# A selective-scan stage rebuilt in tiles of 32 channels by four states

## The chip, the cores and the metric

The kernel runs on one NeuronCore of a Trainium2 chip. The metric is the device time of one launch in microseconds (us). Five engines work side by side, each with its own queue in order: PE (matrix products), DVE (vector), ACT (activations), POOL (GpSimd, a slower vector engine) and SP, which issues the transfers. SBUF is the working memory, PSUM the memory that PE writes.

## What is computed

Four layers follow one another on x of shape (64, 128, 28, 28), in float32. Layer 0: two 3x3 convolutions with quantised weights and batch norms over the whole batch. Layer 1: attention over the 784 positions of each image. Layer 2: a Mamba block per image with 160 inner channels d and 24 states n; it is the part that the change rewrites. Layer 3: a small Mamba block over 8 tokens at each pixel, then a group norm.

```python
# layer 2, per image: seq is (784, 128), normalised over the channels
xz = seq @ W_in.T                       # 160 columns xm, 160 columns z
xm = silu(depthwise_conv(xm, conv_w, 4 taps, causal) + conv_b)
dt, Bm, Cm = split(xm @ W_x.T)          # 8, 24 and 24 columns
delta = softplus(dt @ W_dt.T + b_dt)    # (784, 160)
A = -exp(A_log)                         # (160, 24)
def step(h, inp):                       # h is (160, 24), over 784 positions
    d_t, u_t, B_t, C_t = inp
    h = exp(d_t[..., None] * A) * h + (d_t * u_t)[..., None] * B_t[:, None, :]
    y = einsum('bdn,bn->bd', h, C_t)
    return h, y
y = scan(step) + xm * D
out = (y * silu(z)) @ W_out.T
```

So each image has 160 x 24 = 3840 independent recurrences over 784 positions, which is 30 tiles of 128 partitions.

## The kernel before

`conv_block` runs layer 0 over all images and leaves its result in DRAM. `attention_and_mamba` then goes image by image through layers 1 and 2. `token_mamba` does layer 3 after all images are done. The change is in `attention_and_mamba` and in the host's layout of its weights; `token_mamba` only takes over the helper that keeps the loads of ACT's tables in order.

In `attention_and_mamba` a generator `before(b)` prepares image b: attention (`et`, `x1`), then the norm (`xn`), the input projection (`win`), the depthwise convolution on DVE (lines 400 to 405: four taps of part A with 128 channels, then of part B with the 32 others, which are held four times over in 128 partitions), z, the projection to B, C and dt (`parts`, `dt`), and the softplus that gives `delta` and `du` = delta times u (lines 449 to 461). B and C are split into bf16 parts so that a bf16 product with the 0/1 matrix `sel` can spread one row of them over all 128 partitions exactly.

`scan(b)` walks over 30 pieces: 24 pieces of 128 channels with one state n each, and 6 of 32 channels by four states. Each piece takes an exponential on ACT, a spread of the B row by PE into PSUM (`bb`), the injection and the scan on DVE, a spread of the C row (`cc`), the product with C on DVE, and a sum into `y` by PE:

```python
nc.scalar.activation(a, deltas[i], AF.Exp, scale=A[:, k : k + 1])
product(bb, [(sel[:, k, :], bc[0])])
run(1 if j % 2 else 2)
nc.vector.tensor_tensor(halves(h), halves(dus[i]), bb[:, :, :HT], ALU.mult)
nc.vector.tensor_tensor_scan(h, a, h, 0.0, ALU.mult, ALU.add)
product(cc, [(sel[:, k, :], bc[1])])
nc.vector.tensor_tensor(halves(h), halves(h), cc[:, :, :HT], ALU.mult)
```

`after(b)` multiplies with z on POOL, projects, undoes the four directions of the layer, adds the residue and makes the token projections `utd` and `ztd` for layer 3. While `scan(b)` is written out, `run` places one or two steps of `after(b - 1)` followed by `before(b + 1)` between its pieces. The framework sets each engine's final order from these places, its own ready times and the buffers. PSUM is held by two buffers `bc`, one `side` for everything outside the scan, and one `y`, two banks each.

Of the kernel before, what the change touches and what calls it, by code (L numbers as in the profile page):

```python
# [15 lines left out]
F32 = mybir.dt.float32  # L16
# [7 lines left out]
C = 128  # L24
# [11 lines left out]
    norm_w=1, norm_b=1, cwA=4, cbA=1, bdtA=1, DA=1, cwB=4, cbB=1, bdtB=1, DB=1, scale=1, AlogA=24, AlogB=6,  # L36
# [3 lines left out]
    WqT=16, WkT=16, WvT=128, bv=128, WinT=416, WxA=264, WxB=264, WdtT=256, WoutA=128, WoutB=128, fwT=128,  # L40
)
PK4 = dict(BDx=512, BDt=16, BDo=256, dtw=32, dtb=32, Alog=512)
# [15 lines left out]


COPIES = (0, 64, 96)  # L60
# [7 lines left out]
def tile_kernel(ctx: ExitStack, tc: tile.TileContext, x, w1t, w2t, m2t, vecs, pk3, pk4, out):  # L68
# [23 lines left out]
    last = attention_and_mamba(tc, x, c2d, s2, b2x15, x2d, utd, ztd, pk3, pk4, vec, v, ident, eps)  # L92
    token_mamba(tc, x2d, utd, ztd, pk4, v, ident, eps, out, NB, last)

# [116 lines left out]
def attention_and_mamba(tc, x, c2d, s2, b2x15, x2d, utd, ztd, pk3, pk4, vec, v, ident, eps):  # L211
    nc = tc.nc
    NB = x.shape[0]
    NT, TP = 7, 112
    NS = 24
    NG = 6

    with ExitStack() as ctx:
        wp = ctx.enter_context(tc.tile_pool(name="w3", bufs=1))
        p2 = ctx.enter_context(tc.tile_pool(name="p3", bufs=2))  # L220
        p1 = ctx.enter_context(tc.tile_pool(name="p3b", bufs=1))
        st = ctx.enter_context(tc.tile_pool(name="st3", bufs=3))
        ps = ctx.enter_context(tc.tile_pool(name="ps3", bufs=2, space=PSUM))
        pss = ctx.enter_context(tc.tile_pool(name="pss3", bufs=1, space=PSUM))
        psy = ctx.enter_context(tc.tile_pool(name="psy3", bufs=1, space=PSUM))

        pk = wp.tile([C, NPK3], F32, name="pk")
        nc.sync.dma_start(pk, pk3)
# [5 lines left out]
        def big_psum(p=C):  # L234
            return ps.tile([C, 2, 512], F32, name="bc")[:p]

        def side_psum(p=C):
            return pss.tile([C, 2, 512], F32, name="side")[:p]

# [9 lines left out]
        mean_w = wp.tile([C, C], F32, name="mean_w")  # L249
        nc.vector.memset(mean_w, 1.0 / C)  # L250


        win = wp.tile([C, 416], F32, name="win")
        nc.vector.tensor_scalar(win, w("WinT"), v("norm_w"), None, ALU.mult)
        inb_ps = big_psum()
        for i, (a, b) in enumerate(((0, 128), (128, 256), (256, 384), (384, 416))):
            nc.tensor.matmul(inb_ps[: b - a, 0, i : i + 1], lhsT=w("WinT", a, b), rhs=v("norm_b"), start=True, stop=True)
        inb = wp.tile([C, 4], F32, name="inb")
        nc.vector.tensor_copy(inb[:, 0:3], inb_ps[:, 0, 0:3])
        nc.vector.tensor_copy(inb[:32, 3:4], inb_ps[:32, 0, 3:4])  # L260


        wxc = wp.tile([C, 256], F32, name="wxc")
        nc.sync.dma_start(wxc, pk4[:, TOK_AT["P1"][0] : TOK_AT["P1"][1]])
        wz = wp.tile([C, 256], F32, name="wz")
        nc.sync.dma_start(wz, pk4[:, TOK_AT["P2"][0] : TOK_AT["P2"][1]])
        nc.vector.tensor_mul(wxc, wxc, wz)
        wz = wp.tile([C, 256], F32, name="wz2")
        nc.sync.dma_start(wz, pk4[:, TOK_AT["Wz"][0] : TOK_AT["Wz"][1]])


        a0 = VEC_AT["AlogA"][0]
        A = wp.tile([C, NS + NG], F32, name="A")
        nc.scalar.activation(A, vec[:, a0 : a0 + NS + NG], AF.Exp)
        nc.vector.tensor_scalar(A, A, -1.0, None, ALU.mult)


        eye = wp.tile([C, 32], BF16, name="eye")
        nc.vector.memset(eye, 0.0)
        for p in COPIES:  # L280
            nc.vector.tensor_copy(eye[p : p + 32, :], ident[p : p + 32, p : p + 32])
        sel = wp.tile([C, NS + NG, C], BF16, name="sel")
        nc.vector.tensor_copy(sel[:, :NS, :], eye[:, :NS].unsqueeze(2).broadcast_to([C, NS, C]))
        nc.vector.tensor_copy(
            sel[:, NS:, :].rearrange("p g (r d) -> p (g r) d", r=4),
            eye[:, :NS].unsqueeze(2).broadcast_to([C, NS, 32]),
        )
# [5 lines left out]
        def tmp(name, n=T):  # L293
            return p2.tile([C, n], F32, name=name, tag="tmp", bufs=8)

        def silu_of(dst, src, **kw):
            nc.scalar.activation(dst, src, AF.Silu, **kw)

        def before(b):

            raw = p2.tile([C, T], F32, name="raw")
            nc.sync.dma_start(raw, c2d[b])
            idn = p2.tile([C, T], F32, name="idn")
            nc.sync.dma_start(idn, x[b])
            nc.vector.scalar_tensor_tensor(raw, raw, s2, idn, ALU.mult, ALU.add)
            nc.scalar.activation(raw, raw, AF.Relu, bias=b2x15, scale=15.0)
            nc.vector.tensor_scalar(raw, raw, 15.0, MAGIC, ALU.min, ALU.add)
            x0 = p2.tile([C, T], F32, name="x0")
# [4 lines left out]
            for name, bias in (("WqT", "bq"), ("WkT", "bk")):  # L313
                acc = side_psum(16)
                product(acc, [(w(name), x0)])
                t = p1.tile([16, T], F32, name=name)
                nc.scalar.activation(halves(t), acc[:, :, :HT], AF.Identity, bias=v(bias, p=16))
                qk.append(t)
                yield
            qt, kt = qk  # L320
            vt_ps = side_psum(TP)
# [14 lines left out]
            et = p1.tile([TP, NT, T], F32, name="et")  # L336
            for i in range(NT):
                sc = side_psum(TP)
                product(sc, [(qt[:, i * TP : (i + 1) * TP], kt)])
                nmax = p2.tile([TP, 1], F32, name="nmax")  # L340
                nc.vector.tensor_reduce(nmax, sc[:, :, :HT], AX.XY, ALU.max, negate=True)  # L341
                e = p2.tile([TP, T], F32, name="e")
                den = p2.tile([TP, 1], F32, name="den")
                nc.scalar.activation(halves(e), sc[:, :, :HT], AF.Exp, bias=nmax, accum_out=den)  # L344
# [6 lines left out]
                tr = side_psum(TP)  # L351
                for j in range(NT):
                    nc.tensor.matmul(  # L353
                        tr[:, j // 4, (j % 4) * TP : (j % 4 + 1) * TP],
                        lhsT=e[:, j * TP : (j + 1) * TP], rhs=diag, start=True, stop=True,
                    )
                for h, n in ((0, 4), (1, 3)):
                    nc.scalar.copy(
                        et[:, 4 * h : 4 * h + n, i * TP : (i + 1) * TP],
                        tr[:, h, : n * TP].rearrange("p (j c) -> p j c", c=TP),  # L360
                    )
                yield
            av = side_psum()
            product(av, [(vt[:, j, :], et[:, j, :]) for j in range(NT)])
            x1 = p2.tile([C, T], F32, name="x1", bufs=3)
            nc.vector.scalar_tensor_tensor(halves(x1), av[:, :, :HT], v("att_gamma"), halves(x0), ALU.mult, ALU.add)

            yield
# [4 lines left out]
            nc.scalar.copy(s[0:32], x1[0:32])  # L373
            nc.scalar.copy(s[32:64], x1[32:64, ::-1])
            nc.scalar.copy(s_wh[64:96], swapped[64:96])
            nc.scalar.copy(s_wh[96:128], swapped[96:128, ::-1, ::-1])
            acc = side_psum()
            product(acc, [(mean_w, s)])
            xc = tmp("xc")
            nc.vector.tensor_sub(halves(xc), halves(s), acc[:, :, :HT])  # L380
            yield
            sq = tmp("sq")
            nc.scalar.activation(sq, xc, AF.Square)
# [3 lines left out]
            lnv = tmp("lnv")  # L387
            nc.scalar.activation(halves(lnv), acc[:, :, :HT], AF.Ln, bias=eps)
            nc.scalar.activation(lnv, lnv, AF.Exp, scale=-0.5)
            xn = tmp("xn")  # L390
            nc.gpsimd.tensor_tensor(xn, xc, lnv, ALU.mult)

            yield

            us, zs = [], []
            for i, part in enumerate("AB"):
                acc = side_psum()
                product(acc, [(win[:, i * C : (i + 1) * C], xn)])
                xm = tmp("xm", T + 3)
                nc.vector.memset(xm[:, 0:3], 0.0)  # L400
                nc.scalar.activation(halves(xm[:, 3:]), acc[:, :, :HT], AF.Identity, bias=inb[:, i : i + 1])
                cv = tmp("cv")
                nc.vector.tensor_scalar(cv, xm[:, 0:T], v(f"cw{part}", 0), v(f"cb{part}"), ALU.mult, ALU.add)
                for k in range(1, 4):
                    nc.vector.scalar_tensor_tensor(cv, xm[:, k : k + T], v(f"cw{part}", k), cv, ALU.mult, ALU.add)  # L405
                us.append(cv)
                yield
            for i, (a, n) in enumerate(((256, 128), (384, 32))):
                acc = side_psum(n)
                product(acc, [(win[:, a : a + n], xn)])  # L410
                z = p2.tile([n, T], F32, name=f"z{i}")
                silu_of(halves(z), acc[:, :, :HT], bias=inb[:n, 2 + i : 3 + i])
                zs.append(z)
            yield
            for i in range(2):
                u = p2.tile([C, T], F32, name=f"u{i}")
                silu_of(u, us[i])
                us[i] = u
            uA, uB = us
            srcs = (("WxA", C, uA), ("WxB", 32, uB[:32]))  # L420


# [580 lines left out]
```

## Time and profile before

The time is 19386.77 us, the median of three runs (19373.35 to 19403.07). The profiled execution spans 19390.3 us. Busy time of the engines in it:

| engine | busy us | share of the span |
|---|---|---|
| PE | 15010.2 | 77% |
| DVE | 15343.1 | 79% |
| ACT | 10844.4 | 56% |
| POOL | 6488.9 | 33% |

The scans of layer 2 run from 1122.7 to 12771 us, 64 images one after the other; POOL's time lies nearly all in the token stage after that. In the profile a line such as `L483 DVE TENSOR_TENSOR_SCAN h<-a,h 128x784 f32<-128x784 f32 x1531 | 2790.2, 1822 | 51.4 <-DVE h L482 0.9` reads: code line, engine, operation, the tile written and the tiles read, shapes, count, then the busy time in us, the mean of one in ns, and the time for which the engine stood idle ahead of them with what ended it. A matrix product of float32 appears as two instructions.

### The profile page before, as it was taken

To read this page: it belongs to the slowest core of one execution; us is meant where nothing else is said; L and a number is where in the kernel's file an instruction comes from. 1 tells how busy PE (TensorE), PEld (TensorE's weight loads), DVE (VectorE), ACT (ScalarE), POOL (GpSimd) and SP (SyncE) were. 2 spreads that over 40 slices of the span, in tenths; PEclk is the share of its full clock that TensorE was granted. 3 is DMA by queue.
4 is the path that set the end of the run, shared out by engine and by line. 5 is a ranking of instruction groups with operands and counts; after the bars stand their busy time and mean duration, and the time that the engine had idled before them with its cause. 6 is when DMAs were issued, how large, how long until landed. Compare 5 with 4: busy or idle time off the path is not lost.

```text
span 19390.3 us, 167002 instructions
## 1 busy us (share of the span) xinstructions
PE 15010.2 (77%) x56552; PEld 8571.3 (44%) x56552; DVE 15343.1 (79%) x15415; ACT 10844.4 (56%) x23179; POOL 6488.9 (33%) x3064
## 2 busy tenths in 40 slices
PE   9978888888888888888888888866666666666666
PEld 5533333333333333343333333345555555555554
DVE  1368878878788878888888887778888888888888
ACT  0235445445445445445445455457777777777776
POOL 0001101101101101101001011048888888888887
PEclk9978888888888888888888888888888788887787
DMA  2400000000000000000000000011111111111111
GB/s 75 151 11 16 15 16 16 15 16 16 14 17 17 14 17 17 14 16 18 14 16 18 14 16 15 9 34 50 48 48 50 46 49 50 50 47 47 45 47 45
DMA packets 342632, 605.55 MB, mean 31 GB/s; under 512 B 70416, under 2 KB 188560, under 8 KB 341776
## 3 DMA queue, kind: packets, MB, share of 16 engines
q1 hardware_dynamic: 341776, 594.87, 9.6%
q8 instruction: 448, 7.34, 0.2%
q14 instruction: 408, 3.34, 0.1%
HBM read 363.51 MB, written 231.21 MB: 31 GB/s over the span
## 4 chain that ended last, share of the span: by engine, by line
PE 45%; DVE 26%; ACT 13%; POOL 10%; issue 6%; DMA 1%; SPq 0%; DVEq 0%; POOLq 0%; ACTq 0%
PE side L244 13%; PE y L488 12%; ACT a L627 5%; PE acc L124 5%; DVE h L486 5%; DVE h L483 4%; PE y L823 4%; POOL db L799 4%; PE side L353 4%; PE bc L244 3%; DVE h L482 2%; DVE h L814 2%; DVE a L816 2%; DVE h L818 2%; DVE cv L405 2%
## 5 line engine op out<-in xcount | busy, mean ns | idle before, releaser
L627 ACT ACTIVATE a<-delta,A 128x98 f32<-128x98 f32 x14336 | 3903.3, 365 | 1093.9 <-PE y L823 789.5
L503 POOL TENSOR_TENSOR yo<-yo,z 128x784 f32<-128x784 f32 (+1 forms) x128 | 243.6, 1903 | 10035.4 <-DVE yo L493 10035.4
L799 POOL TENSOR_TENSOR db<-u,BC 128x896 f32<-128x896 f32 x1568 | 3332.4, 2141 | 741.6 <-DVE h L818 600.0
L483 DVE TENSOR_TENSOR_SCAN h<-a,h 128x784 f32<-128x784 f32 x1920 | 3502.2, 1824 | 66.5 <-DVE h L482 0.9
L488 PE MATMUL y<-h,ident 128*128 128x392 f32 x6144 | 2896.9, 592 | 784.4 <-DVE h L486 777.5
L823 PE MATMUL y<-a,ident 128*128 128x280 f32 x7168 | 2152.5, 468 | 1150.5 <-DVE a L816 1142.6
L477 ACT ACTIVATE a<-delta,A 128x784 f32<-128x784 f32 x1920 | 1810.9, 946 | 2102.2 <-DVE h L483 2040.5
L823 PEld LDWEIGHTS y<-a,ident 128*128 128x128 f32 x7168 | 1611.0, 228 | 1697.2 <-POOL db L799 763.1
L486 DVE TENSOR_TENSOR h<-h,bc 128x784 f32<-128x784 f32 x1920 | 1853.9, 966 | 374.3 <-PE bc L244 338.5
L244 PE MATMUL bc<-parts,sel 128*128 128x392 bf16 x7680 | 1878.8, 365 | 314.7 <-DVE h L482 312.1
L482 DVE TENSOR_TENSOR h<-du,bc 128x784 f32<-128x784 f32 x1920 | 1847.2, 962 | 251.0 <-POOL du L461 221.9
L488 PEld LDWEIGHTS y<-h,ident 128*128 128x128 f32 x6144 | 1184.9, 214 | 1844.1 <-DVE h L486 1213.0
L244 PEld LDWEIGHTS <-sel 128*128 128x128 bf16 x7680 | 768.8, 107 | 1801.1 <-issue 1421.2
L814 DVE TENSOR_TENSOR h<-h,a 128x896 f32<-128x896 f32 x1344 | 1473.2, 1096 | 33.4
L818 DVE TENSOR_TENSOR h<-h,db 128x896 f32<-128x896 f32 x1120 | 1227.5, 1096 | 50.4 <-DVE late L816 0.5
L816 DVE TENSOR_TENSOR a<-h,BC 128x896 f32<-128x896 f32 x896 | 974.3, 1087 | 20.6
L341 DVE TENSOR_REDUCE nmax<-side 112x1 f32<-112x784 f32 x448 | 436.6, 975 | 565.0 <-PE side L244 565.0
L353 PE MATMUL side<-diag,e 112*112 112x112 f32 x6272 | 747.1, 274 | 163.5 <-DVE diag L348 163.5
L353 PEld LDWEIGHTS side<-diag,e 112*112 112x112 f32 x6272 | 739.8, 191 | 279.2 <-issue 236.5
L825 PEld LDWEIGHTS y<-late,ident 128*128 128x128 f32 x7168 | 836.2, 192 | 40.6 <-DVE late L816 21.4
L825 PE MATMUL y<-late,ident 128*128 128x112 f32 x7168 | 837.1, 274 | 15.0 <-DVE late L816 15.0
L344 ACT ACTIVATE e<-side,nmax 112x784 f32<-112x784 f32 x448 | 409.6, 914 | 778.5 <-DVE nmax L341 778.5
(200 smaller groups left out, 23300.6 us busy)
## 6 DMA issues: line engine op xcount, KB each, us to landing
utd<-tok SPq DMA_DIRECT2D x128, 392.0 KB, 2.3
ztd<-tok SPq DMA_DIRECT2D x128, 392.0 KB, 2.3
rows<-utd SPq DMA_DIRECT2D x192, 256.0 KB, 2.9
xt<-in_x SPq DMA_DIRECT2D x32, 784.0 KB, 5.2
c1d<-raw SPq DMA_DIRECT2D x32, 784.0 KB, 6.3
xt<-c1d SPq DMA_DIRECT2D x32, 784.0 KB, 5.6
c2d<-raw SPq DMA_DIRECT2D x64, 392.0 KB, 4.3
raw<-c2d SPq DMA_DIRECT2D x64, 392.0 KB, 3.1
```

Of the source, the lines that this page charges most:

```text
L244: nc.tensor.matmul(dst[:, h, :HT], lhsT=lhsT, rhs=rhs[:, h * HT : (h + 1) * HT], start=(i == 0), stop=(i == len(terms) - 1),)
L353: nc.tensor.matmul(tr[:, j // 4, (j % 4) * TP : (j % 4 + 1) * TP], lhsT=e[:, j * TP : (j + 1) * TP], rhs=diag, start=True, stop=True,)
L477: nc.scalar.activation(a, deltas[i], AF.Exp, scale=A[:, k : k + 1])
L482: nc.vector.tensor_tensor(halves(h), halves(dus[i]), bb[:, :, :HT], ALU.mult)
L483: nc.vector.tensor_tensor_scan(h, a, h, 0.0, ALU.mult, ALU.add)
L486: nc.vector.tensor_tensor(halves(h), halves(h), cc[:, :, :HT], ALU.mult)
L488: nc.tensor.matmul(y[:, hf, :HT], lhsT=red, rhs=h[:, hf * HT : (hf + 1) * HT], start=(j == 0), stop=(j == count - 1),)
L627: ins = nc.scalar.activation(*args, **kw)
L799: nc.gpsimd.tensor_tensor(x, of_dg(du[:, t, ds, :]), BC[:, t, :NS, :].unsqueeze(1).broadcast_to([C, DB, NS, G]), ALU.mult)
L814: nc.vector.tensor_tensor(h, h, flat(at(t)), ALU.mult)
L823: nc.tensor.matmul(y3[:, 1:6], lhsT=ident, rhs=a[:, 0:5, :, n, :], start=False, stop=False)
L825: nc.tensor.matmul(y3[:, 6:8], lhsT=ident, rhs=late[:, :, :, n, :], start=False, stop=(n == NS - 1))
```

## The change

- **Pieces.** All 160 channels are now cut into five quarters q of 32 channels, and the 24 states into six groups g of four. A piece (g, q) holds 32 channels by four states in 128 partitions: 30 pieces, as before.
- **Rows by transfers.** `dbc` (B and C) and delta and du are stored to DRAM (`bcd`, `dud`), and read back spread: `rows_bc` reads each of four rows of B (or C) into 32 partitions, `rows_d` reads one quarter of delta (or du) four times. Each tile takes four transfers. The products with `sel` and the bf16 splitting are gone.
- **Engines.** The injection du times B is on POOL for every piece. The product with C is on POOL for q = 1 and 3, on DVE for the rest. For q = 2 and 4 the decay `a` lies in PSUM and the scan writes over it; for q = 0 the scan's result lies in PSUM; for q = 1 and 3 all is in SBUF. The one PSUM buffer `ah` serves q = 0, 2 and 4.
- **Sum over states.** `fold` (128 x 32) sums the four states; quarter q < 4 goes to partitions 32q of `y`. The fifth quarter is cut into four runs of 196 positions, which take the four partition groups; part B is from here on a (128 x 196) tile.
- **Convolution.** The depthwise taps are multiplied into the input projection (`taps`), so that four shifted products accumulate in PSUM; the first three columns are corrected by `bias`.
- **Attention.** It has a PSUM buffer of its own (`att`) and runs two images ahead (`attend`), with its output product cut into seven; `prepare` runs the rest one image ahead. Loads of ACT's tables are grouped (`Tables.use`).

The core of the diff:

```diff
+        def spread(tile, src):
+            for r in range(4):
+                nc.sync.dma_start(tile[32 * r : 32 * r + 32], src(r))
...
+                t = p2.tile([C, T], F32, name=f"{name}r", bufs=2)
+                n = 24 * k + 4 * g
+                spread(t, lambda r: bcd[n + r : n + r + 1, :].broadcast_to([32, T]))
...
+                t = p2.tile([C, T], F32, name=name, bufs=NQ + 1)
+                spread(t, lambda r: dud[k, 32 * q : 32 * q + 32, :])
...
-                    nc.scalar.activation(a, deltas[i], AF.Exp, scale=A[:, k : k + 1])
-                    bb = big_psum()
-                    product(bb, [(sel[:, k, :], bc[0])])
-                    run(1 if j % 2 else 2)
-                    h = st.tile([C, T], F32, name="h")
-                    nc.vector.tensor_tensor(halves(h), halves(dus[i]), bb[:, :, :HT], ALU.mult)
-                    nc.vector.tensor_tensor_scan(h, a, h, 0.0, ALU.mult, ALU.add)
-                    cc = big_psum()
-                    product(cc, [(sel[:, k, :], bc[1])])
-                    nc.vector.tensor_tensor(halves(h), halves(h), cc[:, :, :HT], ALU.mult)
...
+                for q in range(NQ):
+                    delta, du = d_rows[q]
+                    k = g * NQ + q
+                    h = st.tile([C, T], F32, name="h", bufs=7)
+                    nc.gpsimd.tensor_tensor(h, du, Bg, ALU.mult)
+                    if q in (2, 4):
+                        a = psh.tile([C, 1024], F32, name="ah")[:, :T]
+                        state = a
+                    else:
+                        a = st.tile([C, T], F32, name="a")
+                        state = h if q % 2 else psh.tile([C, 1024], F32, name="ah")[:, :T]
+                    act(a, delta, AF.Exp, scale=A[:, k : k + 1])
+                    nc.vector.tensor_tensor_scan(state, a, h, 0.0, ALU.mult, ALU.add)
+                    run()
+                    (nc.gpsimd if q % 2 else nc.vector).tensor_tensor(h, state, Cg, ALU.mult)
+                    hs.append(h)
...
+                for hf in range(2):
+                    for q in range(4):
                         nc.tensor.matmul(
...
+                            y[32 * q : 32 * q + 32, hf, :HT], lhsT=fold, rhs=hs[q][:, hf * HT : (hf + 1) * HT],
+                            start=first, stop=False, skip_group_check=True,
                         )
...
+            shifted = [xn[:, k : k + T] for k in range(4)]
+            uB_ps = side_psum()
+            quarters(uB_ps[:, 0, :QT], [(taps[:, k, C:], shifted[k]) for k in range(4)])
...
+            uA_ps = side_psum()
+            product(uA_ps, [(taps[:, k, :C], shifted[k]) for k in range(4)])
...
+                for m, src in enumerate((pos, ab)):
+                    if i == 0:
+                        nc.sync.dma_start(dud[m, :C], src)
...
+            def run():
+                nonlocal count
+                if count % 2 == 0:
+                    next(one, None)
+                next(two, None)
+                count += 1
```

## The prediction

> **What bounds the kernel now.** I first cut the span into stages by the first and last start of the lines that belong to one of them (the answer for single lines), then asked for the busy time of every engine in each stretch:
>
> ```profile
> core 0: us, PE busy (x) PEld busy (x) DVE busy (x) ACT busy (x) POOL busy (x), PEclk, DMA share, GB/s
> 0.00:946.00 946.00, 915.69 (x3456) 552.20 (x3456) 206.10 (x343) 162.64 (x165) 1.42 (x8) 0.99 0.34 111
> 946.00:1122.00 176.00, 106.40 (x248) 51.80 (x249) 50.12 (x84) 47.80 (x64) 4.82 (x3) 0.55 0.11 38
> 1122.00:12771.00 11649.00, 9549.73 (x31731) 4435.88 (x31731) 9358.55 (x9279) 5755.12 (x6771) 1159.14 (x573) 0.88 0.04 15
> ...
> 12804.00:19390.00 6586.00, 4423.20 (x21088) 3525.92 (x21088) 5724.11 (x5701) 4869.27 (x16169) 5321.70 (x2480) 0.80 0.16 48
> ```
>
> Convolutions take 946 us, a lead-in 176, the 64 scans 11,649 (182.0 per image), the tail up to the token stage 33, the token stage 6586. The change touches only the middle 11,858. There PE and DVE are each busy 80 to 82% and POOL 10%: two engines share the bound. The groups of the stage (window 2500 to 11,800, which is 51 images) say with what:
>
> ```profile
> L483 DVE TENSOR_TENSOR_SCAN h<-a,h 128x784 f32<-128x784 f32 x1531 | 2790.2, 1822 | 51.4 <-DVE h L482 0.9 <-ACT a L477 0.5
> L488 PE MATMUL y<-h,ident 128*128 128x392 f32 x4897 | 2310.4, 592 | 607.8 <-DVE h L486 601.8
> L244 PE MATMUL bc<-parts,sel 128*128 128x392 bf16 x6124 | 1502.0, 366 | 250.9 <-DVE h L482 250.9
> L486 DVE TENSOR_TENSOR h<-h,bc 128x784 f32<-128x784 f32 x1531 | 1478.1, 965 | 252.3 <-PE bc L244 225.4 <-DVE h L483 0.9 <-DVE diag L348 0.6
> L482 DVE TENSOR_TENSOR h<-du,bc 128x784 f32<-128x784 f32 x1531 | 1472.9, 962 | 201.4 <-POOL du L461 175.9 <-PE bc L244 22.3
> ```
>
> Per image, DVE spends 2790/51 = 54.7 us on scans and 28.9 + 29.0 on the two products, 112.5 of its 147; PE spends 29.5 us (1502/51) spreading B and C rows, 54.8 summing y. The last view is the order of time at an image boundary, where POOL and DVE run together:
>
> ```profile
> 1858.42 1.85 POOL L458 TENSOR_TENSOR pos<-pos,ab 128x784 f32<-128x784 f32 x1
> 1859.57 2.35 DVE L483 TENSOR_TENSOR_SCAN h<-a,h 128x784 f32<-128x784 f32 x1
> 1860.35 3.20 POOL L459 TENSOR_TENSOR delta<-w,pos 128x784 f32<-128x784 f32 x1
> ```
>
> The scan (1.79 median) took 2.35 and ended 1.65 us after the POOL product did; the next POOL product took 3.20 and ended 1.63 after the scan. They took turns. L482, which reads one operand in PSUM, kept its 0.97 beside POOL.
>
> **What the skill says.** "SBUF — State Buffer", section "Who interferes with whom": a DVE instruction with two SBUF inputs contends with a GpSimd one that reads SBUF, one with at most one SBUF input does not. The lines above agree. "GPSIMD Engine Reference", section 3.1: a GpSimd product is about twice as slow as DVE's; here 1.85 against 0.97. "DMA: Bandwidth & Descriptors", section "Anatomy of one DMA — SWDGE (gpsimd) path": about 2 us fixed per transfer on that path; here SP's 128 KB land in 2.1. "TensorEngine Tiling (Array Packing)", "Key Properties": column tiles can work in parallel; no trace here shows it, since the fold products of before all use one tile.
>
> **The change, part by part, per image.** There are 30 (128 x 784) pieces before and after (24 + 6; 6 groups of 5), so scans and exponentials keep their count.
>
> DVE: the 30 injections leave (-28.9), 12 of 30 C products leave (-11.6). The depthwise convolution goes (2 x (0.69 + 3 x 1.03) = -7.5), the bf16 splitting of B and C (-5.0), the dt copy (-1.0); part B's softplus works on 196 columns (-2.8); seven short x1 pieces for one long one, and bias fix-ups, +1.5. Its own work falls to 30 x 1.79 + 18 x 0.97 = 71.1, plus 19.4 for the rest: 90. Whether a scan with operands in PSUM costs other than 1.79 the trace doesn't show; the PSUM product costs what the SBUF one does, so I take 1.79, with 0 to +0.5 us on each of 18 (up to +9).
>
> POOL: 30 injections and 12 C products at 1.85 = 77.7; xn, three softplus steps, y times z for part A, 5 x 1.85 = 9.3; part B's quarters (196 columns) some 2. Sum 89, against 18 now.
>
> The shared port: all of POOL's 89, plus the DVE scans whose a and h both lie in SBUF (q = 0, 1, 3: 18 x 1.65 = 29.7), plus DVE's other such work and its fast tensor_scalars (raw, x0, w, ab, diag: 6), less some 0.2 for each of 18 turns to POOL (-3.6): 121 us that can't overlap. The scans q = 2, 4 read a from PSUM and the DVE C products read the state there, so these 39 us run beside POOL.
>
> PE: spreading goes (-29.5); y by 96 fold passes of 392 columns at 0.395 (now 484/1224) and 96 of 98 columns at 0.14 gives 51 for 54.8; seven short attention products for a long one +2; the convolution as four taps and quarters +9; x_proj without row copies -7.4; dt and out projections -4.6. The groups of before add to 161 where the stretch has 150 (they overlap), so 161 - 34.3 = 127 is scaled to 118.
>
> ACT: 30 exponentials (28.4) stay; convolution biases go, four table loads for six, about 78 for 91. It isn't near the bound.
>
> DMA on SP's queue: 88 spreads of 100 KB, 10 DRAM stores of delta and u, one of B and C, for nothing before; at 0.32 us of issue 32 us of SP, and 10 MB per image, some 70 GB/s where the convolution stage moved 111. Rows are asked for one group (over 20 us) ahead and land in about 2.1, so I cost them at nothing in steady state. Behind an SP wait for a late delta lie the attention loads and the next B and C rows; bounds: 0, or one round trip of 2.3 + 2.1 us and a first injection, 6 us per image, if delta comes last.
>
> Waits added: a POOL C product waits for its scan with the next injections behind it; h has 7 buffers and a group holds 5 until its y products, so POOL runs two injections ahead. The PSUM buffer of decays is one, used by q = 0, 2, 4; between two uses lies a scan of q = 1 or 3, which hides the exponential.
>
> Sum: three engines are loaded almost alike: port 121, PE 118, DVE 90 plus up to 30 of blocking. Before, the busiest reached 150 of 182 = 82%. With that share PE gives 118/0.82 = 144 and the port 147; I take 144. Outside the loop: the lead-in now holds two attentions, +100 (176 now covers one attention and one input chain, on a PE clock of 0.55); the last two images lack an attention beside them, -40; tail 35. So 176 + 100 - 40 + 35 + 64 x 144 = 9487 for 11,858: -2371. Convolution and token stages are the same instructions. The profiled span is 19,390.3; the three timed runs, 19,373 to 19,403 with median 19,387, stand round it, so 19,390 - 2371 - 3 = 17,016, rounded to 17,020.
>
> **The rivals.**
> 1. Column tiles overlap and queues fall well: the fold passes cost half, PE drops to about 97, the port is nearly full: 128 per image, 271 + 8192 = 8463, time 15,990. For it: q = 0..3 go to four column groups in turn. Against: no such overlap is seen, and DVE must meet PE and ACT in every attention step (nmax waited 425 us on PE in the window).
> 2. Three coupled queues reach less than 82%: 74% of 118 gives 160, time 18,040. For it: DVE blocked by POOL also blocks the products behind it that need no port, and each 1.85 us POOL product delays PE's y. PE's clock falls in gaps (0.55 in the lead-in).
> 3. Slower: the hand-over chain. Image b+1's inputs follow image b-1's output projection inside one scan; gate, output, fusion, token projections, norm, taps, x_proj, softplus, DRAM and back are about 92 us of work by these rows (28 + 64) over some 44 changes of engine. A mean wait of h at each gives 92 + 44h, which h = 1.2 puts at 145. The period equals today's at (11,858 - 271)/64 = 181.0, that is from h = 2.0 on; at h = 2.1, 184 us and 19,580. For it: every queue is in order and POOL's mean queue is full. Against: input chains go by in 182 us today beside a busier PE.
> 4. The change doesn't do what it says: if PSUM operands didn't free the port, 12 more scans and 18 products enter it (+37), 158 per image even at full packing, 170 likely, time 18,680. The L482 line speaks against it; I count it within cases 2 and 3.
>
> **How the numbers follow.** Forecast 0.55, case 1 0.17, case 2 0.19, case 3 0.09. Faster by over 0.2% (39 us, about what a measurement of this kernel can tell from no change) takes the first three but for 0.01: 0.90; within 0.2% 0.01; slower 0.09. The range runs from 126 per image (271 + 8064, time 15,870: the port at 96%) to 166 (10,895, time 18,430: PSUM scans at their dear end with case 2), which leaves out about 2 in 10.
>
> **What would show it.** Right: an image period of 135 to 153 in the exponentials of A; POOL busy (blocked time included) 75 to 88% of the scan stretch, injections of 1.85 at the least and over 2.2 on average; scans of q = 0, 1, 3 stretched above 1.79 and those of q = 2, 4 not; PE's spreading gone; the other stages within 20 us of 946 and 6586. Wrong: injections at 1.85 on average (no blocking), first injections of an image waiting for DMA by 5 us or more, scan stretches with POOL below 65% busy (the chain of hand-overs decides), or fold passes well below 0.33 us apiece.

## The result and the profile after

The changed kernel takes 19504.6 us (median of four runs, 19497.47 to 19516.3) where the kernel before took 19383.15 beside it: 1.0062 of its time, 95% interval 1.0045 to 1.0079. The forecast was 17,020, with 15,870 to 18,430 as its range. The measured time lies outside the range, above it, and a little above the time before.

The stages come from the busy time of each engine in stretches of time, with the columns of the table of before (span 19500.9 us):

```profile
946.00:1202.00 256.00, 157.53 (x608) 105.76 (x608) 47.66 (x116) 60.36 (x95) 10.64 (x9) 0.58 0.08 26
1202.00:12879.00 11677.00, 7687.61 (x35348) 4103.63 (x35348) 6843.14 (x6000) 4517.52 (x6169) 6608.60 (x3318) 0.67 0.24 70
12879.00:19500.00 6621.00, 4441.05 (x21120) 3532.40 (x21120) 5736.27 (x5711) 4878.68 (x16182) 5319.35 (x2482) 0.80 0.16 48
```

The lead-in grew by 80 us (256 for 176) and the end of the program stayed. The scans take 11,677 us, 182.5 per image, hardly other than the 182.0 of before. Yet the work did get smaller: PE's busy time in the stretch fell from 9550 to 7688 us, DVE's from 9359 to 6843, ACT's from 5755 to 4518. No engine is busy for more than 66% of it, and PE's clock fell from 0.88 to 0.67. The expected gain turned into waiting.

The groups with the most time (code line, engine, names, count, then busy us, mean ns of one, and the idle time ahead of them with what ended it):

```profile
L590 POOL TENSOR_TENSOR h<-ur,Br 128x784 f32<-128x784 f32 x1920 | 4167.2, 2192 | 2985.1 <-PE y L613 1465.0
L606 PE MATMUL y<-h,fold 128*32 128x392 f32 x6144 | 1690.5, 690 | 1334.3 <-DVE h L600 1021.5
L598 DVE TENSOR_TENSOR_SCAN h<-a,h 128x784 f32<-128x784 f32 x768 | 1933.3, 2523 | 357.3 <-POOL h L590 294.4
L598 DVE TENSOR_TENSOR_SCAN ah<-ah,h 128x784 f32<-128x784 f32 x768 | 1373.0, 1788 | 1059.0 <-ACT ah L226 584.3
L226 ACT ACTIVATE ah<-dr,A 128x784 f32<-128x784 f32 x768 | 702.2, 914 | 2538.5 <-DVE h L600 2535.0
```

The shared port shows as forecast: a scan with operands and result in SBUF takes 2.52 us on average, one with its result alone in PSUM 2.12, one with its decays in PSUM 1.79. Injections on POOL take 2.19. New is the idle time: POOL, which should have been nearly full, waits 2985 us ahead of its injections, most of it for the y products that give the h buffers back; ACT's exponentials into `ah` wait 2539 us.

`yA`, the sum over states for part A, is written once per image, when its last piece is done. In the order of time of one image (5045.7 to 5230.0, from one yA to the next) and the start of the one after it, three stretches stand out in which DVE runs no scan. The first lies at the change of images. DVE, from the last scan of one image to the first of the next:

```profile
5226.28 1.80 DVE L598 TENSOR_TENSOR_SCAN ah<-ah,h 128x784 f32<-128x784 f32 x1 [1.05 <-ACT ah L226]
...
5229.99 1.03 DVE L618 SCALAR_TENSOR_TENSOR yA<-uA,vec,y 128x784 f32<-128x784 f32 x1 [0.90 <-PE y L613]
...
5239.85 0.86 DVE L641 COPY r<-side 32x392 f32<-32x392 f32 x1 [8.51 <-ACT r L226]
5242.15 0.86 DVE L641 COPY r<-side 32x392 f32<-32x392 f32 x1 [1.44 <-ACT r L226]
5246.15 1.03 DVE L646 SCALAR_TENSOR_TENSOR x<-side,vec,x 128x784 f32<-128x784 f32 x1 [3.14 <-PE side L340]
5247.10 1.79 DVE L598 TENSOR_TENSOR_SCAN ah<-a,h 128x784 f32<-128x784 f32 x1
```

The stop is 19.0 us (5228.08 to 5247.10). The first scan carries no wait of its own: in DVE's queue it stands behind the output steps of the image before (`r`, `x2`), and these wait for ACT and PE in turn. The injection that it needs had been ready since 5236.8. In the same time SP issues the rows of the next image, one transfer after the other:

```profile
5223.39 1.71 SPq L545 DMA_DIRECT2D dud<-pos  x4
...
5228.86 1.81 SPq L553 DMA_DIRECT2D dr<-dud  x4
5230.72 1.81 SPq L553 DMA_DIRECT2D ur<-dud  x4
...
5250.28 1.75 SPq L553 DMA_DIRECT2D Cr<-bcd  x4
```

A tile's four transfers hold SP's queue for 1.8 us, the burst of dud stores and rows 29 us (5223.4 to 5252.0).

The longest stop has nothing to do with rows. DVE, and then ACT, some 50 us after yA:

```profile
5279.58 1.78 DVE L598 TENSOR_TENSOR_SCAN ah<-ah,h 128x784 f32<-128x784 f32 x1
...
5293.21 1.16 DVE L411 TENSOR_TENSOR vt<-att,pk 112x512 f32<-112x512 f32 x2 [9.26 <-PE att L405]
...
5306.02 0.33 DVE L451 SCALAR_TENSOR_TENSOR x<-att,vec,x 128x112 f32<-128x112 f32 x1 [7.41 <-PE att L449]
...
5318.89 1.80 DVE L598 TENSOR_TENSOR_SCAN ah<-ah,h 128x784 f32<-128x784 f32 x1 [6.97 <-ACT ah L226]
```

```profile
5310.40 0.91 ACT L226 ACTIVATE e<-att,nmax 112x784 f32<-112x784 f32 x1 [7.80 <-DVE nmax L423]
...
5311.43 1.28 ACT L233 ACT_TABLE_LOAD   x1
...
5317.86 0.92 ACT L226 ACTIVATE ah<-dr,A 128x784 f32<-128x784 f32 x1
```

For 37.5 us DVE, PE and ACT hand the attention of another image to and fro; the exponential that the scan needs stands in ACT's queue behind two attention exponentials, the Silu block and its two table loads. A third stop of 18.3 us (5169.9 to 5188.2) is like it. Each of the three comes once per image, and together they make 75 us of the 184.3. The rest is 109.5 us for all 30 pieces; gaps of 3 to 6 us between scans, 24 us in all, are still in it.

### The profile page after: what moved, and what is told of

It reads as the page before. It is cut to its first block, busy times and chain, and to the rows that moved or that the text cites. A ratio compares the mean times of both kernels' runs of the same rounds, so it can differ in the third digit from the quotient of the medians.

```text
span 19500.9 us, 183056 instructions
## 1 busy us (share of the span) xinstructions
PE 13200.8 (68%) x60532; PEld 8293.8 (43%) x60532; DVE 12833.6 (66%) x12169; ACT 9620.3 (49%) x22612; POOL 11940.1 (61%) x5816
## 4 chain that ended last, share of the span: by engine, by line
PE 24%; POOL 19%; DVE 19%; ACT 13%; issue 12%; SPq 5%; DMA 2%; POOLq 0%; DVEq 0%; ACTq 0%
POOL h L590 7%; ACT a L226 6%; SPq L553 5%; PE att L340 4%; POOL db L920 4%; PE side L340 4%; PE y L944 4%; DVE h L598 3%; DVE ah L598 2%; DVE h L935 2%; PE att L436 2%; PE att L449 2%; DVE h L939 2%; DVE a L937 2%; ACT s L226 1%
## 5 line engine op out<-in xcount | busy, mean ns | idle before, releaser
L590 POOL TENSOR_TENSOR h<-ur,Br 128x784 f32<-128x784 f32 x1920 | 4167.2, 2192 | 2985.1 <-PE y L613 1465.0
L600 POOL TENSOR_TENSOR h<-h,Cr 128x784 f32<-128x784 f32 x768 | 1649.6, 2155 | 1723.6 <-DVE h L598 1464.0
L606 PE MATMUL y<-h,fold 128*32 128x392 f32 x6144 | 1690.5, 690 | 1334.3 <-DVE h L600 1021.5
L598 DVE TENSOR_TENSOR_SCAN h<-a,h 128x784 f32<-128x784 f32 x768 | 1933.3, 2523 | 357.3 <-POOL h L590 294.4
L598 DVE TENSOR_TENSOR_SCAN ah<-ah,h 128x784 f32<-128x784 f32 x768 | 1373.0, 1788 | 1059.0 <-ACT ah L226 584.3
L436 PE MATMUL att<-diag,e 112*112 112x112 f32 x6272 | 1082.4, 350 | 741.5 <-DVE diag L431 736.9
L226 ACT ACTIVATE a<-dr,A 128x784 f32<-128x784 f32 x1152 | 1047.5, 940 | 728.8 <-DVE h L598 691.4
L449 PE MATMUL att<-et,vt 112*128 112x112 f32 x6272 | 1104.1, 346 | 315.9 <-ACT et L226 315.9
L449 PEld LDWEIGHTS att<-et,vt 112*128 112x128 f32 x6272 | 1018.9, 252 | 499.3 <-ACT et L226 478.0
L600 DVE TENSOR_TENSOR h<-ah,Cr 128x784 f32<-128x784 f32 x1152 | 1112.4, 966 | 18.4
```

The costliest lines, as they stand in the source:

```text
L226: ins = self.tc.nc.scalar.activation(*args, **kw)
L436: nc.tensor.matmul(tr[:, j // 4, (j % 4) * TP : (j % 4 + 1) * TP], lhsT=e[:, j * TP : (j + 1) * TP], rhs=diag, start=True, stop=True,)
L449: nc.tensor.matmul(av, lhsT=vt[:, j, :], rhs=et[:, j, :], start=(j == 0), stop=(j == NT - 1))
L590: nc.gpsimd.tensor_tensor(h, du, Bg, ALU.mult)
L598: nc.vector.tensor_tensor_scan(state, a, h, 0.0, ALU.mult, ALU.add)
L600: (nc.gpsimd if q % 2 else nc.vector).tensor_tensor(h, state, Cg, ALU.mult)
```

## The experiments

"Per image" is the time from the first yA to the last, over 63. The kernel before runs at 182.0 per image (scan stretch over 64), the changed one at 182.8. Several executions of one kernel differed by at most 0.2%; all experiments but e10, e15 and e19 are one execution each, and the differences read from them are larger by far.

| run | edit to the changed kernel | us | per image |
|---|---|---|---|
| changed | none | 19504.6 | 182.8 |
| e1_merged | one transfer per tile, 4 x 32 rows | 18975.2 | 173.7 |
| e2_nosilu | no Silu | 19046.9 | 172.9 |
| e3_both | e1 and e2 | 19170.6 | 174.9 |
| e4_free | exponentials not held to a table's block | 18518.9 | 167.5 |
| e5_scan_only | scan, output, rows alone | 16111.0 | 129.8 |
| e6_no_att | without attention | 17201.3 | 146.6 |
| e7_inputs_first | e4, inputs ahead of outputs | 18914.0 | 174.0 |
| e8_merged16 | one transfer per tile, 32 x 4 rows | 17438.6 | 150.0 |
| e10_merged_free | e8 and e4 | 19161.7 | 177.9 |
| e11_d_merged | e8's tiles for delta and du alone | 18643.3 | 169.2 |
| e12_bc_merged | e8's tiles for B and C alone | 18457.5 | 166.0 |
| e13_c_dve | e10, all C products on DVE | 18401.3 | 165.8 |
| e15_merged16_again | e8 | 17429.1 | 149.9 |
| e16_scan_only_merged | e8 and e5 | 15791.5 | 124.5 |
| e17_pace_merged | e8, another pace of `prepare` | 18767.7 | 171.0 |
| e18_pace | another pace of `prepare` | 18371.0 | 164.8 |
| e19_tie0 | first scan ahead of the output steps | 19500.7 | 182.7 |

**One suspect at a time.** The first theory was that the burst and the table blocks each cost their stop. e1 joins the four transfers of a tile:

```diff
-            for r in range(4):
-                nc.sync.dma_start(tile[32 * r : 32 * r + 32], src(r))
+            nc.sync.dma_start(tile, src)
...
-                spread(t, lambda r: dud[k, 32 * q : 32 * q + 32, :])
+                spread(t, dud[k, 32 * q : 32 * q + 32, :].unsqueeze(0).broadcast_to([4, 32, T]))
```

> The changed kernel with one transfer where it has four for each spread tile (22 instead of 88 per image) and two instead of eight for part B's delta and du; the bytes are the same. Theory A (at the image boundary the scan waits for SP, which issues some 60 transfers of 0.46 us one after the other): the boundary shrinks by about 20 us, the period from 184 to 160 to 168, the time to about 18,200 (17,900 to 18,500). Theory B (the fences round ACT's table loads hold the scan's exponentials back twice per image) alone: the gap at the boundary is refilled by the next fence, period 180 or more, time above 19,200. Theory C (many short hand-overs, none of them decisive): the same as B.

e2 turns the eight Silu activations into Identity and drops the table blocks (`tables.use`), e3 does both:

> The changed kernel with the eight Silu of layer 2 per image replaced by Identity (so the activation is left out) and with the four table loads and their ordering taken away. Theory B: the two standstills of the scan (18 and 37 us per image in the profile of the change) go, period 130 to 145, time 16,100 to 17,000. Theory A alone: at most the four loads go, period 176 to 182, time 19,000 to 19,400. Theory C: some 10 us less, period about 174, time 18,900.

> Merged transfers and no Silu and no table loads together. Theories A and B together: the period comes down to what the shared port and PE allow, 112 to 128, time 14,900 to 15,900. Theory C: over 150, time over 17,300.

Each brought some 9 to 10 us per image, and both together no more (7.9): they don't add. e1 lies between what its theories had put; e2 and e3 fit the third, many short hand-overs. And e1 was not the experiment that it was meant to be, for its transfers get slow when several follow one another. SP's queue in it:

```profile
5039.99 0.56 SPq L549 DMA_DIRECT2D dr<-dud  x1
...
5044.57 3.62 SPq L549 DMA_DIRECT2D dr<-dud  x1
5048.24 3.72 SPq L549 DMA_DIRECT2D ur<-dud  x1
...
5052.62 7.98 SPq L549 DMA_DIRECT2D ur<-dud  x1
```

e4 writes the scan's exponentials as `nc.scalar.activation(...)` for `act(...)`, so that they are no longer kept in order with the loads of tables:

> The changed kernel in which only the scan's 30 exponentials per image are freed from the ordering against the table loads (where one falls between the Silu, the table is loaded once more, 2 x 1.28 us); all results are as in the changed kernel. Theory B: the scan goes on during the Silu stretches, period 140 to 160, time 16,700 to 18,000. Theory A: no change beyond 3 us per image, time 19,300 to 19,700. Theory C: no change.

It brought 15 us per image, between what the theories had put.

**The chains.** e5 and e6 leave out input chain and attention, or attention alone, for all but the first images. The edit to attention is the same in both:

```diff
-            if b < NB:
-                x1s[b] = yield from attention(b)
+            if b < 2:
+                x1s[b] = kept[b] = yield from attention(b)
+            elif b < NB:
+                x1s[b] = kept[b % 2]
+                yield
```

> The changed kernel with layer 2's input chain left out but for image 0 and attention left out but for images 0 and 1: every image scans image 0's rows (the transfers stay) and runs the output side (gate, projections, token projections). Theory D (the queues in a fixed order tie the scan to the attention and input chains): alone the scan comes down to the shared port, about 106 us of it per image, period 108 to 130, time 14,600 to 16,100. Rival P (the injections on POOL, the shared port and the spread transfers hold the scan itself near today's period): 155 or more, time 17,600 or more.

> The changed kernel with attention left out but for images 0 and 1 (all later images take one of their results); input chain, scan and output side are whole. If attention's hand-overs are what holds the scan: period 125 to 145, time 15,700 to 17,000. If it is the input chain with its way through DRAM at the image boundary: 160 to 180, time 17,900 to 19,200.

The scan with its output side takes 129.8 us per image; the input chain adds 17, attention 36; e6 thus came a little above the range put for attention. Attention isn't on the scan's path by its data: it runs two images ahead. What it costs comes by the queues and engines that they share.

e7 puts the input chain ahead of the rest of the output chain (on e4's base), to give the next image's delta more time:

```diff
+                rest = after(b - 1, given.pop(b - 1), ys)
+                yield next(rest)
...
+            yield from rest
```

> As e4_free (the scan's exponentials not ordered against the table loads), and within one image's scan the input chain of the next image is placed ahead of the output side of the last one, whose gate product alone stays first. All results are as in the changed kernel. If the late end of the input chain sets the gap at the boundary (delta is stored only as the scan ends): rows are there before the scan ends, 15 to 30 us per image less than e4_free, time 16,600 to 17,600. If not: within 3 us per image of e4_free, 18,300 to 18,700.

A miss: 174.0, slower than e4's 167.5. An earlier delta isn't what was lacking.

**The transfers.** e8 gives the partitions of a piece the order channel-major, so that a tile comes in one transfer whose slowest dimension is 32 (`fold` and the layout of A follow it):

```diff
-                spread(t, lambda r: dud[k, 32 * q : 32 * q + 32, :])
+                spread(t, dud[k, 32 * q : 32 * q + 32, :].unsqueeze(1).broadcast_to([32, 4, T]))
```

> The changed kernel with one transfer for each spread tile, as e1_merged, but with the partitions of a tile ordered by d and then by n, so that the transfer's outermost count is 32 instead of 4 (in e1_merged a 392 KB transfer took some 3.8 us each, one after the other). If e1_merged gained little because its transfers got slow: the boundary shrinks by some 20 us, time 17,900 to 18,500. If the boundary doesn't matter: as e1_merged, 18,800 to 19,200.

It gave 150.0, less than either theory had put. SP's queue, with the same tiles as in e1:

```profile
5133.47 0.56 SPq L548 DMA_DIRECT2D dr<-dud  x1
5134.12 0.55 SPq L548 DMA_DIRECT2D ur<-dud  x1
```

e1 and e8 are the cleanest pair of the study: in both, but for the set-up of `fold`, the instructions of PE, ACT, DVE and POOL stand in the same sequence (of PE's 39,412 records 14 stand a few places off), and both move the same bytes in as many transfers. Only the shape differs. The first transfers of a burst hold the queue equally long (0.56 us), the later ones 3.7 us or 0.6 to 1.1; the burst lasts 37 us in e1 (5038.7 to 5075.9) and 10 in e8 (5132.1 to 5142.3). That is worth 23.7 us per image. The waits of the injections for `ur` (engine and line that wait, whom for, us in 6000, times, longest), e1 and then e8:

```profile
POOL h L586 <- DMA ur<-dud: 774.7, 160, 11.4
POOL h L585 <- DMA ur<-dud: 126.5, 51, 6.3
```

Per image these are 22 us and 3 us. The Trainium skill has a reason that fits, "DMA: Bandwidth & Descriptors", section "Why a DMA increments its semaphore by 16 and not by 1": a transfer is shared out over as many DMA engines, 16 at most, as divide the slowest dimension of both sides; by this rule four there, sixteen here. The durations in a burst agree with it; no view here shows how many engines worked, and a transfer of e1 that came alone held the queue for no more than 0.51 us (median of `Br`).

e10 then adds e4's edit to e8, which should have been better still:

> e8_merged16 and e4_free together: one transfer for each spread tile, and the scan's exponentials not ordered against the table loads. If the two standstills lie in different places: their gains (32 and 15 us per image) add up, period 133 to 139, time 16,300 to 16,800. If they are one gap seen from two sides: 147 to 152, time 17,200 to 17,600.

It was the largest miss: 19161.7 us (ratio to the kernel before 0.9882, 0.9866 to 0.9899), 28 us per image slower than e8 with the same transfers and, but for 16 more table loads in the whole run, the same instructions. What differs is the sequence in the queues. One wait of it shows how:

```profile
POOL yA L624 <- DVE rden L428: 715.1, 33, 23.0
```

Once per image the product with z on POOL waits up to 23 us, for the most part because yA on DVE, and the last passes of its sum on PE, stand behind steps of attention and of the input chain.

e11 and e12 join the transfers of delta and du, or of B and C, alone; the other rows come in four transfers of 8 channels:

> As e8_merged16, but B's and C's rows are again read with four transfers for each tile (of 32 partitions each); delta's and du's with one. If it is the burst at the image boundary that costs (40 of delta and du behind the last store): nearly all of e8_merged16's gain stays, period 150 to 160, time 17,400 to 18,100. If SP's transfers cost all along the scan: half of it, 165 to 172, time 18,400 to 18,850.

> The other half: B's and C's rows with one transfer for each tile, delta's and du's with four. If the burst at the boundary costs: most of the gain is lost, period 170 to 182, time 18,700 to 19,450. If transfers cost all along the scan: 165 to 172, time 18,400 to 18,850.

e13 is e10 with POOL's 12 C products on DVE:

> e10_merged_free with all 30 products with C on DVE, none on POOL: 22 us per image less for POOL and for the shared port, 12 more for DVE. If the port or POOL sets the period by now: 5 to 15 us per image less than e10_merged_free, 300 to 1000 us. If the order of the queues sets it: within 4 us per image (250 us) either way.

They gain 13.6, 16.8 and (on e10) 12 us per image; e11 and e12 both came into the range put for transfers that cost all along the scan. e11's queues stand nearly as in the changed kernel (compared by name within an image, 96 to 98% of the instructions of DVE, ACT and POOL keep their sequence): the stop between images falls from 19.0 to 7.2 us, the two others stay (36.7 and 17.8). But among the few instructions that moved are the first two scans of an image, which now stand ahead of `r`; so at this stop rows and order changed together. Nor is either run a clean half: the transfers left at four per tile hold SP for 0.64 us each (median), where those of the changed kernel hold it for 0.42. e12's sequence is another (54% for DVE, 65% for ACT, 77% for POOL), so its gain can't be put down to the transfers.

**The order by itself.** e15 repeats e8, e16 takes the scan alone on e8's base, and e17 and e18 change nothing but the pace at which `prepare` is written between the pieces:

```diff
-                if count % 2 == 0:
-                    next(one, None)
+                next(one, None)
```

> The kernel of e8_merged16 once more, with an interval. If e8's time is its own: 17,440 us within 0.3%, about 0.90 of the kernel before. If it was one lucky execution: nearer to the 19,160 of e10_merged_free, which issues the same instructions in another order.

> One transfer per spread tile, and input chain for image 0 alone, attention for images 0 and 1 alone (their work is left out for the other images, whose scans reuse image 0's rows). e5_scan_only had 129.8 us per image with four transfers per tile. If the scan then stands on its loads (port estimated at 121, fold passes 96 x 0.275 = 26) and the burst at the image boundary costs what it seems to (some 20 us): 106 to 122 per image, 14,600 to 15,600 us in all. If the burst costs nothing where no other chain waits: 128 to 131, about 16,100.

> e8_merged16 with the prepare chain stepped at every run() instead of every other one: no instruction more or less, only its place in the queues. If the order of the queues sets the period: it moves by 5 us per image or more, either way (17,100 or less, or 17,800 or more). If transfers set it: 150 per image as in e8, 17,440 within 0.5%.

> The changed kernel with the prepare chain stepped at every run(), nothing else changed, four transfers per tile as they are. If the order of the queues sets the period: it moves by 5 us per image or more from 182.8 (19,180 or less, or 19,830 or more). If the burst of 88 transfers sets it: 19,500 within 0.5%.

e15 confirms e8: 17429.1 us, 0.899 of the kernel before (0.8977 to 0.9002), the fastest of the study. Its stretch of scans:

```profile
1202.00:10810.00 9608.00, 6834.73 (x35346) 3780.26 (x35346) 6791.76 (x5997) 4523.69 (x6166) 6730.28 (x3316) 0.76 0.25 85
```

PE now reaches 71%, at a clock of 0.76. The same edit of the pace slows e8 by 21 us per image (e17) and speeds the changed kernel up by 18 (e18), with not an instruction more or less. In e17 the wait is this one:

```profile
POOL h L595 <- DVE h L593: 1505.5, 245, 19.9
```

POOL's C products wait for scans that stand behind other chains; in e15 this wait is 501.7 us. e16 fell a little outside what either theory gave: 124.5, 5 less than e5. Where no other chain waits, joining the transfers is worth little.

**The stop between images.** e19 makes the product with z, and all that follows it, come after the first scan of the next image; the added instruction leaves the values as they are:

```diff
+                    if g == 0 and q == 0 and z is not None:
+                        nc.vector.scalar_tensor_tensor(
+                            z[:, 0:1], state[:, 0:1], 0.0, z[:, 0:1], ALU.mult, ALU.add
+                        )
```

> One instruction more per image: after the first scan of image b, DVE rewrites one column of z of image b - 1 with its own value plus 0 times the scan's result, so that the product with z, the output projection and the r and x2 steps of image b - 1 come after that scan in every queue, where they stood ahead of it. All transfers stay as in the changed kernel. If the place in the queue makes the stop at the boundary: the scan can run some 9 us earlier (its injection was done at 5236.8, it ran at 5247.1), period 170 to 176 us for 182.8, 18,700 to 19,080 in all. If the burst of transfers makes it: 182 to 183, 19,450 to 19,550. If the chain from the output of one image to the inputs of the next sets the period: that chain starts some 4 to 8 us later, so 183 to 190, 19,500 to 19,960.

19500.7 us (1.006, 1.0043 to 1.0077): no gain. The number is the one that the burst was to give, but the trace shows something else. DVE at the change of images:

```profile
5040.12 1.80 DVE L598 TENSOR_TENSOR_SCAN ah<-a,h 128x784 f32<-128x784 f32 x1 [5.83 <-POOL h L590]
...
5051.76 0.85 DVE L645 COPY r<-side 32x392 f32<-32x392 f32 x1 [8.65 <-ACT r L226]
5054.06 0.85 DVE L645 COPY r<-side 32x392 f32<-32x392 f32 x1 [1.44 <-ACT r L226]
5054.94 1.79 DVE L598 TENSOR_TENSOR_SCAN h<-a,h 128x784 f32<-128x784 f32 x1
```

The first scan now waits 5.83 us for its injection, which itself waited 3.29 us for the rows, and runs 7 us after yA, not 17; the second one stands behind `r` in its place and comes 22 us after yA, where it was 20. The stop was split, not removed. So here an earlier place in the queue doesn't help without earlier rows. Nor would earlier rows alone have moved the first scan of the changed kernel, whose injection was done 10 us ahead of it; no run has them alone. e8 and e11 have both. In e8 the framework, presumably because it reckons with earlier rows, put the first scan even ahead of yA:

```profile
5135.52 1.79 DVE L593 TENSOR_TENSOR_SCAN ah<-ah,h 128x784 f32<-128x784 f32 x1
...
5140.91 1.80 DVE L593 TENSOR_TENSOR_SCAN ah<-a,h 128x784 f32<-128x784 f32 x1 [2.59 <-POOL h L585]
5142.62 1.01 DVE L613 SCALAR_TENSOR_TENSOR yA<-uA,vec,y 128x784 f32<-128x784 f32 x1
```

A stop of 3.6 us for 19.0. And e8's longest one is 18.7 for 37.5: its attention starts ahead of yA (the first step on DVE 13 us before it, not 48 us after), and `vt` and the first `nmax`, which stood in the stop, run between scans. With the same sequence but slow transfers (e1) this stop is 22.

## Why the prediction was wrong, step by step

**Work and port: right in the sums, on PE by luck.** The forecast had PE at 118 us per image and POOL at 89 plus blocking; the stretch of scans gives 120.1 (7687.61/64) and 103.3. On PE two errors cancel: the sum over states takes 32 us ((1690.5 + 364.3)/64) where 51 was put, and everything else at least 88 where 76 was (127 less 51, ahead of the scaling to 118), at a clock of 0.67 where it had been 0.88. The Trainium skill, "SBUF — State Buffer", section "Who interferes with whom", was used for the port, and holds: 2.52 us against 1.79 for the two kinds of scan, and 966 ns for DVE's products with an operand in PSUM. Rival 4 falls. Fold passes take 0.275 us apiece (1690.5/6144), below the 0.33 named for rival 1: the column groups overlap in part. The time that this saved on PE is no longer what decides. The lead-in grew by 80 where 100 was put. Of the forecast's own signs of being wrong two came: these passes, and POOL busy for 57% of the stretch (6608.6 of 11,677), which it had read as hand-overs deciding. Two did not: injections took 2.19 us on average, and the first one of the image shown waited 1.43 us for DMA.

**The failing step: "With that share PE gives 118/0.82 = 144".** The share at which three queues overlap was carried over from the kernel before as if it belonged to the machine. It belongs to one sequence of instructions: 65.7% here (120.1 of 182.8), 71% in e15, and between e8 and e10, with equal work, 150.0 and 177.9 us per image. 144 was not out of reach: 150 came. But the forecast had no term for the stops, and they are 75 us of the image shown, against 36 + 4 in e8. Outside of them the changed kernel takes 109.5 us, e8 some 110 (150.4 less 18.7, 17.6 and 3.6), e11 109 (170.9 less 36.7, 17.8 and 7.2), e6 110 (146.8 less 21.2, 8.9 and 7.0). Between the changed kernel and e6 the stops account for the whole of what attention costs. The 110 us are a little under the forecast's loads of 118 and 121, some of which is done within the stops. This division doesn't serve for all runs: with every stop over 6 us taken out, e2, e3, e4 and e10 are left with 120 to 129.

**"I cost them at nothing in steady state", with bounds of 0 and 6 us: wrong.** In that step an SP wait was thought to hold up one round trip. But the rows of a whole image are asked for at once when its delta is there, and each 98 KB transfer holds SP for some 0.45 us (1.81/4, where 0.32 was put), so the last tile comes 20 us after the first. With the sequence held, the speed of the transfers is worth 23.7 us per image (e1 to e8), and joining those of delta and du 13.6 with the sequence nearly held but for two scans at the stop itself (e11). From the changed kernel to e8 it is 32.8, of which the shorter stop in attention (18.8) is for the most part a matter of sequence (e1, with e8's sequence and slow transfers, has 22). Alone, beside no other chain, joining saves 5.3 (e5 to e16).

**"Between two uses lies a scan of q = 1 or 3, which hides the exponential": wrong.** This counted the buffer and forgot the queue. The exponential can't start until the buffer is free, and by then attention and Silu steps stand ahead of it on ACT. The longest stop, 37.5 us, ends with this wait; in the third, of 18.3, the exponential is done 1 us ahead of the scan, which stands behind a step of attention on DVE as well. e2 and e4 take parts of it away (10 and 15 us per image, through changed sequences too).

**Rival 3** had the slower side and the size (equal at 181.0 per image; 182.8 came). Its one loop, from an image's output to the inputs of the next but one, isn't shown to be the cause: e19 starts that chain some 9 us later (`x2` comes 25 us after yA, where it came 16 after) and the period stays at 182.7, and e7, which shortens the way to delta, got slower than its base. What holds is the idea below it: hand-overs between in-order queues, of attention more than of the input chain (36 and 17 us by e5 and e6), with the scan behind them. **Rival 2** had the falling clock (0.67) and too high a share.

**What stays open.** The buffer `ah` is single, and ACT's wait for it to come free is the longest in its queue (2535 us); no run gives it a second one. Why one sequence takes 150 and another 178 is shown stop by stop for some of them, not from a rule; none of the runs gives a way to forecast the period of a sequence without running it. How much of e12's and e13's gains is sequence was not separated.

## What to carry to other kernels

If several chains share in-order queues and none of the engines is full, don't scale the busiest engine by the share of another program: walk through one period and ask, for each instruction of the critical chain, what stands ahead of it and for whom that waits. Count transfers as issue time on their queue, and mind their shape: with a slowest dimension of 4 for 32 the burst was 27 us longer here, and the image 23.7. And take no small experiment at its face value before its sequence is compared with the original's: here a changed pace alone moved the time by 18 to 21 us per image, as much as most edits.

## What the runs showed of the hardware

In a burst, a 392 KB transfer with a slowest dimension of 4 held SP's queue for 0.5 to 0.8 us at first and for up to 8 us later on, most often 3.6 to 3.8 (e1); one with 32 for 0.5 to 1.3 (e8). Alone, one with 4 held it for 0.51. A quarter of it (98 KB) from 32 rows held it for some 0.45, from 8 channels four times over for 0.64 (e11). Fold passes of 392 columns in four column groups took 0.275 us on average at a clock of 0.67, and 0.230 at 0.76 (1413.7/6144 in e15), against 0.395 in one group before. PE's granted clock in the scans was 0.67 where PE was busy 66% of the time, 0.76 at 71%, 0.88 at 82%; the busy share alone doesn't set it, for the token stage of the changed kernel had 0.80 at 67% (4441.05 of 6621).
